# The places at which put-off layer-norm pieces are summed, moved to a list of 16 groups

## The chip, the cores and the metric

The kernel runs on one core of a Trainium2 chip. The metric is the device time of one execution in microseconds; the median of several runs counts. Lower is better.

## The reference, cut to what matters

Two layers are applied to four images of 64 x 64 tokens with 256 channels, in float32. Layer 0 is self-attention over the 4096 tokens of an image with 32 score channels and 128 value channels, a projection back and a residual. Layer 1 is an attention over triangles of token pairs, with 8 heads, then a residual with layer norm, an MLP with 512 hidden channels and a second layer norm.

```python
def _L0_conv_ref(x, Wf, bf, Wg, bg, Wh, bh, Wo, bo):
    f = xt @ Wf + bf
    g = xt @ Wg + bg
    v = xt @ Wh + bh
    s = jnp.einsum('bqd,bkd->bqk', g, f)
    beta = jax.nn.softmax(s, axis=-1)
    o = jnp.einsum('bqk,bkd->bqd', beta, v)
    o = o @ Wo + bo
    return x + o.reshape(b, h, w, c)

def _L1_conv_ref(...):
    ...
    out = jnp.einsum('biljh,bilhd,bljhd->bijhd', att, v1, v2)
    attn_out = out.reshape(B, N, N, E) @ Wo
    h = x_in + attn_out
    h = _layer_norm(h, ln_agg_g, ln_agg_b)
    mlp = jax.nn.relu(h @ W1 + b1) @ W2 + b2
    h = mlp + h
    return _layer_norm(h, ln_out_g, ln_out_b)
```

The change concerns the last two lines for images 0 and 1: the sum `mlp + h` and the layer norm after it.

## The kernel before

**Order of images.** `run` goes through images b = 0 to 3. For each it does layer 0 (`layer0`) and then layer 1 (`first_layer1` for image 0, `next_layer1` for the others). The order of instructions is the order in which the program issues them; each engine works off its own queue in that order, and an instruction waits at the head of its queue for semaphores of other engines. PE is TensorE, DVE is VectorE, ACT is ScalarE, POOL is GpSimd, SP is SyncE, which issues most DMAs.

**Put-off pieces.** Layer 1's tail (projection, layer norm, MLP) is done in pieces of 256 tokens, 16 an image (`NP`). While layer 1 of image b runs, the pieces of image b - 1 go through the matmuls of the tail. For images 0 and 1 the last part is put off: `carried_off` and `summed_off` store h and the MLP's output z in a DRAM tile `raw` (512 KB a piece, both together), and layer 0 of the image after next (b = 2 or 3) takes them up again. The last part of a piece has six steps, all methods of `Tokens`:

- `recall`: a tile `hz` in the ring of tag "R" (three buffers) is filled from `raw` by a DMA on SP (L1107).
- `settle`: on DVE, h times a row, plus a row, plus z (L1112 to L1114, 128 x 512 each), and statistics (L1185, L1186).
- `rooted`: on ACT, two small activations for one over the root (L1213, L1215).
- `polished`: on DVE, four small instructions that make scale and bias `rn` (L1225 to L1228).
- `scaled`: on ACT, two activations of 128 x 256 (L1247).
- `finish`: on POOL, two products of 128 x 512 (L1337, L1338), then the store to the output on SP (L1339).

**Layer 0.** The queries of an image are eight blocks (`qb`) of 512; the keys eight groups (`k`) of 512. The loop runs over 64 groups of scores g = 8 qb + k. In each group `values(g)` interleaves on PE four score matmuls of group g + 1 (L559, into pairs of PSUM banks; two pairs in all) with four o matmuls of group g (L586). ACT makes the exponentials of the scores in two instructions of 128 x 1024 (L571) into a buffer `e` (tag "k8", two buffers). DVE adds e to a running sum `esum` (L593; a copy, L591, where k = 0). At k = 7 DVE folds the sum together (L596 to L603) and splits it into two parts, `part`, in the ring of tag "hid" (one buffer).

The work on block qb - 1 is spread over the groups of block qb by a table `parts`: at k = 0 `norm` (den matmul on PE, L611; reciprocal on DVE, L615; `oT`, L617) and `bounds` (two reductions, L625), at k = 1 `output` (y, L639, and its stores), later the projections for layer 1, with copies on ACT (L672, L681, L706) into the ring of tag "st" and stores on SP. In image 3 `turn_y` follows at k = 5: eight transposes on DVE (L651) into a buffer of tag "hid", and four stores (L654).

The six steps of the put-off pieces come last in a group, and only where `b > 1`. Their places before:

```python
if b > 1:
    first = 3 * qb if qb < 2 else 2 + 2 * qb
    for t in range(3 if qb < 2 else 2 if qb < last else 0):
        for do, at in (
            (rest.recall, t), (rest.settle, 2 + t + t // 2), (rest.rooted, 3 + t + t // 2),
            (rest.polished, 4 + t + t // 2), (rest.scaled, 5 + t + t // 2), (rest.finish, 7),
        ):
            if k == min(at, 7):
                do(NP * (b - 2) + first + t)
```

So blocks 0 and 1 have three pieces each, settled at k = 2, 3 and 5, and blocks 2 to 6 two each, settled at k = 2 and 3.

Of the kernel before, what the change touches and what calls it, by code (L numbers as in the profile page):

```python
# [29 lines left out]
NP = T // 256  # L30
# [15 lines left out]
    A15/2 R00/1 A17/2 T10/2 A14/2 sp/1 R02/1 sa R05/1 e0/1 R01/1 z0/1 rr/1 T11/2 z1/1 pp/1 e1/1 so/1 A00/1 A05/1  # L46
    R07/1 W1/1 A02/1 A01/1 fa S1 ht V1/1 S0 hU hT
""".split()


ORDER_LAST = """
# [23 lines left out]
def attention_then_triangle_kernel(  # L75
# [99 lines left out]
    def add_b2():  # L175
        b2_bc = work.tile([P, C], F32, tag="st", name="b2_bc", bufs=3)
        nc.gpsimd.dma_start(out=b2_bc, in_=b2.partition_broadcast(P))
        nc.gpsimd.tensor_tensor(lb2_bc, lb2_bc, b2_bc, ALU.add)
        nc.gpsimd.tensor_tensor(lab2_sb, lab2_sb, lab_sb, ALU.add)
# [19 lines left out]
    def fold_bias():  # L199
        ps = pb("fold")  # L200
        for cc in range(2):
            nc.tensor.matmul(ps[:, cc : cc + 1], wo0_sb[:, 0, ts(cc, P)], bh_sb, start=True, stop=True)
        nc.vector.tensor_tensor(bo_sb, bo_sb, ps[:, 0:2], ALU.add)
# [7 lines left out]
    def limits(b):  # L211
        for j, op in enumerate((ALU.min, ALU.max)):
            nc.vector.tensor_reduce(lims[:, j, b : b + 1], dens, AX.X, op)
# [124 lines left out]
    class Ahead:  # L338
# [30 lines left out]
        def load(self, s):  # L369
            if s < self.n:  # L370
                for cc, (tag, bufs) in enumerate((("hT", 2), ("st", 3))):
                    t = self.xT[s, cc] = work.tile([P, 512], F32, tag=tag, name="xT", bufs=bufs)
                    nc.sync.dma_start(out=t, in_=self.d[1 + s // 8]["x"][ts(cc, P), ts(s % 8, 512)])
# [130 lines left out]
    def layer0(b, F, safe, rest, ahead):  # L504
# [14 lines left out]
        def max_piece(qc, t, mx):  # L519
            ps = pb("mxp")  # L520
            nc.tensor.matmul(ps, gT[qc // 16][:, ts(qc % 16, P)], fT[t // 4][:, ts(t % 4, 512)], start=True, stop=True)
            nc.vector.tensor_reduce(mx[:, qc % 4, t : t + 1], ps, AX.X, ALU.max)


        def max_row(mx):
            m = small.tile([P, 4], F32, tag="m", name="m")
            nc.vector.tensor_reduce(m, mx, AX.X, ALU.max)
            ps = pb("row")
            for n in range(4):
                nc.tensor.matmul(  # L530
                    ps[:, ts(n, P)], m[:, n : n + 1].to_broadcast([P, P]), ident, start=True, stop=True
                )
            row = work.tile([P, QB], BF16, tag="attP", name="row")
            nc.scalar.mul(row, ps, -1.0)
            return row

        def pieces(qb):
            mx = small.tile([P, 4, 8], F32, tag="mx", name="mx", bufs=2)
            return mx, [(qb * 4 + n, t) for n in range(4) for t in range(8)]
# [89 lines left out]
        def y(qb, cc):  # L629
            return yT[cc][:, ts(qb, QB)] if qb < last else stage[2][:, 2 + cc, :]  # L630
# [15 lines left out]
        def turn_y(qb, **where):  # L646
            t = work.tile([P, 16, 2, 32], F32, name="yr", **where)
            for cc in range(2):
                rows = y(qb, cc).rearrange("p (k t) -> p k t", t=32)
                for k in range(4):  # L650
                    nc.vector.transpose(t[:, ts(k, 4), cc, :], rows[:, ts(k, 4), :])  # L651
            def kept():
                for r in range(4):
                    nc.sync.dma_start(  # L654
                        out=io["yt"][ts(qb, QB), ts(r, 64)].rearrange("(k t) c -> t k c", t=32),
                        in_=t[ts(r, 32)].rearrange("t k h c -> t k (h c)"),
                    )
            return kept
# [5 lines left out]
        def proj(qb, name, m, ps=None, st=None, queue=nc.sync):  # L664
            col, rows = ts(qb, QB), ts(m, P)
            w = {"q": wq_sb, "k": wk_sb, "v2": wv2_sb}[name]
            ps = pb("proj") if ps is None else ps
            for cc in range(2):
                nc.tensor.matmul(ps, w[:, cc, rows], y(qb, cc), start=(cc == 0), stop=(cc == 1))  # L669
            st = staged(st)  # L670
            if name == "q":
                nc.scalar.mul(  # L672
                    st.rearrange("p (o i l) -> p i o l", o=2, l=32),
                    ps.rearrange("p (i o l) -> p i o l", o=2, l=32), scale1,
                )
                queue.dma_start(
                    out=io["q"][rows, :, ts(qb, 8), :].rearrange("c o i l -> c o (i l)"),
                    in_=st.rearrange("p (o x) -> p o x", o=2),
                )
                return  # L680
            nc.scalar.copy(st, ps)  # L681
            if name == "k":
                queue.dma_start(out=io["k"][rows, col], in_=st)
            else:
                queue.dma_start(
                    out=io["v2"][ts(qb, 8), rows, :].rearrange("l c j -> c l j"),
                    in_=st.rearrange("p (l j) -> p l j", j=N),
                )
# [8 lines left out]
        def proj1(qb, m, ps=None, st=None, queue=nc.sync):  # L697
            ps = pb("v1p") if ps is None else ps
            for n in range(2):
                for cc in range(2):  # L700
                    nc.tensor.matmul(  # L701
                        ps[:, ts(n, C)], y(qb, cc)[:, ts(m * 2 + n, P)], wv1_sb[:, cc, :],
                        start=(cc == 0), stop=(cc == 1),
                    )
            st = staged(st)
            nc.scalar.copy(st, ps)  # L706
            queue.dma_start(
                out=io["v1"][ts(qb * 2 + m, 256), :].rearrange("(n p) c -> p n c", p=P),
                in_=st.rearrange("p (n c) -> p n c", n=2),
            )  # L710
# [3 lines left out]
        def proj_qk(qk, st):  # L714
# [26 lines left out]
        parts = [  # L741
            [norm, bounds],
            [output],
            [lambda qb: proj(qb, "q", 0)],
            [lambda qb: proj(qb, "k", 0), lambda qb: proj(qb, "v2", 0)],
            [lambda qb: proj1(qb, 0)],
            [lambda qb: proj1(qb, 1), lambda qb: proj(qb, "q", 1)],
            [lambda qb: proj(qb, "k", 1)],
            [lambda qb: proj(qb, "v2", 1)],
# [5 lines left out]
            parts[6] = [lambda qb: proj(qb, "q", 1)]  # L755
            parts[7] = [lambda qb: proj(qb, "k", 1)]
        if turned_ahead(b):
            parts[5].append(lambda qb: turn_y(qb, tag="hid", bufs=1)())
        last = NQB - 1
        for r in range(4):  # L760
            score(0, r)
        for g in range(8 * NQB):
            qb, k = divmod(g, 8)
            if b == 0 and not safe:
                for load in later[3 * g : 3 * g + 3]:
                    load()
                if g == 6:
                    fold_bias()
                if g == 20:
                    add_b2()  # L770
            if safe and k == 0 and qb + 1 < NQB:
                mx, todo = pieces(qb + 1)
                for qc, t in todo:
                    max_piece(qc, t, mx)
                row[qb + 1] = max_row(mx)
            values(g, g + 1 < 8 * NQB)

            if qb > 0 and not (qb == last and k >= 6 + late):
                for part in parts[k]:
                    part(qb - 1)  # L780
            if late and g % 2 == 0 and 0 <= g // 2 - 2 < ahead.n:
                ahead.bring(g // 2 - 2)
            if late and g % 2 == 1 and 0 <= g // 2 - 3 < ahead.n:
                ahead.turn(g // 2 - 3)
            if b > 1:
                first = 3 * qb if qb < 2 else 2 + 2 * qb
                for t in range(3 if qb < 2 else 2 if qb < last else 0):
                    for do, at in (
                        (rest.recall, t), (rest.settle, 2 + t + t // 2), (rest.rooted, 3 + t + t // 2),
                        (rest.polished, 4 + t + t // 2), (rest.scaled, 5 + t + t // 2), (rest.finish, 7),  # L790
                    ):
                        if k == min(at, 7):
                            do(NP * (b - 2) + first + t)
            if g == 1 and b > 0 and not safe:
                limits(b - 1)
            if qb == last and k == 3:
                L.fetch_v1(0)
                L.fetch_v1(1)
            if qb == last and k == 5:
                if b > 0:  # L800
                    rest.load(NP * (b - 1))
                L.fetch_qk(0, True)
# [277 lines left out]
    def turned_ahead(b):  # L1080
        return b == NB - 1
# [652 lines left out]
```

## Time and profile before

| | |
|---|---|
| Median of 3 runs (lowest to highest) | 3637.06 us (3630.78 to 3638.11) |
| Time of the profiled execution | 3637.93 us |
| Its span, first to last instruction | 3636.1 us |
| Mean granted clock of TensorE | 0.993 |
| Busy: PE, DVE, ACT, POOL | 97%, 79%, 53%, 49% of the span |
| First to last o matmul (L586) of layer 0: images 0, 1, 2, 3 | 365.7, 386.9, 395.8, 394.4 us |
| settle's first instruction (L1112) | 32 times, median 685 ns, longest 1771 ns |
| finish on POOL (L1337, L1338) | 32 times each, medians 1279 and 1275 ns, longest 1805 and 3296 ns |

The span is the profiled execution's; the runs are timed without a profile. Busy shares are means over stages that differ, so the stage in which the changed code runs has to be read by itself: layer 0 of image 2 (its o matmuls from 1732.5 us on) and of image 3 (from 2600.9 us on). Image 1's layer 0 (from 872.7 us on) has the same matmuls and no put-off pieces.

### The profile page before, as it was taken

The page shows a single profiled execution, that of the slowest core. Times are in us where ns is not written, and L with a number is a line of the kernel's source. Part 1 is how long each engine was busy: PE and PEld are TensorE (multiplying, and loading weights), DVE is VectorE, ACT ScalarE, POOL GpSimd, SP SyncE. Part 2 cuts the span into 40 slices and gives each one's busy share as a digit, 9 for nine tenths or more (in the row PEclk, how much of TensorE's full clock was granted, in tenths as well). Part 3 has the DMA queues.
Part 4 walks back from the last instruction along what each step waited for, and adds up shares of the span by engine and source line. Part 5 has one row for each costly group of instructions (what it writes and reads, how often), then busy time and mean ns, then how long its engine had stood idle before and what let it go on. Part 6 is the DMA issues. An engine that isn't in the chain of part 4 may idle for free.

```text
span 3636.1 us, 58663 instructions
## 1 busy us (share of the span) xinstructions
PE 3521.2 (97%) x22218; PEld 1888.1 (52%) x22218; DVE 2862.1 (79%) x2662; ACT 1922.6 (53%) x4221; POOL 1770.2 (49%) x904
## 2 busy tenths in 40 slices
PE   9999999988999999999999999999899999999998
PEld 6555444434555555554455555554445555555477
DVE  4777499996555569999776649999887766999987
ACT  3444455544444366665444446666444446777655
POOL 5000199995000068989111118889611105999920
PEclk9999999999999999999999999999999999999999
DMA  9444555465111354425422254343623236431221
GB/s 175 140 129 124 138 148 142 117 138 130 50 52 49 90 137 107 104 65 107 112 90 85 75 142 112 85 107 73 138 93 99 90 92 152 97 92 50 66 69 57
DMA packets 509492, 374.37 MB, mean 103 GB/s; under 512 B 320080, under 2 KB 450896, under 8 KB 500368
## 3 DMA queue, kind: packets, MB, share of 16 engines
q1 hardware_dynamic: 460160, 343.56, 34.3%
q0 software_dynamic: 36160, 19.94, 5.4%
q10 hardware_dynamic: 12880, 7.01, 0.6%
q8 instruction: 178, 2.92, 0.3%
q14 instruction: 114, 0.93, 0.1%
HBM read 205.73 MB, written 164.63 MB: 102 GB/s over the span
## 4 chain that ended last, share of the span: by engine, by line
PE 64%; DVE 9%; POOL 6%; issue 4%; ACT 2%; DMA 2%; SPq 0%; ACTq 0%; DVEq 0%; POOLq 0%
PE acc L1052 17%; PE o L586 16%; PE proj L669 6%; POOL Rp L1042 6%; PE zp L1323 4%; PE s L559 4%; PE mp L1303 4%; DVE R L1042 4%; PE sp L940 3%; PE v1p L701 2%; PE hp L1160 2%; PE y L638 1%; PE att L994 1%; DVE esum L593 1%; DVE st L1185 1%
## 5 line engine op out<-in xcount | busy, mean ns | idle before, releaser
L1042 POOL TENSOR_TENSOR Rp<-attP,v 128x2048 f32<-128x2048 f32 x328 | 1491.5, 4578 | 410.1 <-ACT attP L1002 366.9
L1042 DVE TENSOR_TENSOR R<-att,v 128x2048 f32<-128x2048 f32 x696 | 1546.2, 2278 | 68.1 <-PE acc L1052 49.5
L586 PE MATMUL o<-e,v 128*128 128x512 f32 x2048 | 1046.9, 594 | 0.0
L593 DVE TENSOR_TENSOR esum<-esum,e 128x2048 f32<-128x2048 f32 x224 | 513.4, 2292 | 386.4 <-ACT e L571 384.5
L571 ACT ACTIVATE e<-s 128x1024 f32<-128x1024 f32 x512 | 522.4, 1023 | 539.8 <-PE s L559 436.8
L559 PE MATMUL s<-gT,fT 128*128 128x512 f32 x1024 | 786.0, 769 | 18.4 <-ACT e L571 14.8
L1052 PE MATMUL acc<-R,wsel 128*32 128x512 f32 x5568 | 706.8, 603 | 26.9 <-DVE R L1042 19.8
L586 PEld LDWEIGHTS o<-e,v 128*128 128x128 f32 x2048 | 388.7, 190 | 276.6 <-issue 233.9
L1062 ACT COPY ao<-acc 128x1024 f32<-128x1024 f32 x256 | 256.5, 1013 | 290.9 <-PE acc L1052 205.8
L1052 PE MATMUL acc<-Rp,wsel 128*32 128x512 f32 x2624 | 344.4, 596 | 22.8 <-POOL Rp L1042 20.3
L1052 PEld LDWEIGHTS acc<-R,wsel 128*32 128x32 f32 x5568 | 156.0, 110 | 396.2 <-issue 277.1
L1337 POOL TENSOR_TENSOR hz<-hz,log_bc 128x512 f32<-128x512 f32 x32 | 44.7, 1397 | 602.7 <-ACT hz L1247 602.7
L559 PEld LDWEIGHTS s<-gT,fT 128*128 128x128 f32 x1024 | 194.5, 190 | 258.7 <-issue 230.3
L977 ACT ACTIVATE es<-S,rd 128x64 f32<-128x64 f32 x1024 | 258.3, 337 | 15.0 <-DVE rd L969 13.1
L1231 POOL TENSOR_SCALAR nt<-mv 128x2 f32<-128x2 f32 (+1 forms) x49 | 9.4, 192 | 524.0 <-DVE mv L1186 518.9
L1303 PE MATMUL mp<-hT,w 128*128 128x256 f32 x1024 | 244.8, 384 | 1.7 <-ACT hT L1275 1.7
L1323 PE MATMUL zp<-w,hid 128*128 128x256 f32 x1024 | 240.0, 385 | 2.5 <-ACT hid L1312 2.1
L1323 PEld LDWEIGHTS zp<-w,hid 128*128 128x128 f32 x1024 | 187.9, 190 | 50.1 <-issue 14.7
L1303 PEld LDWEIGHTS mp<-hT,w 128*128 128x128 f32 x1024 | 185.1, 190 | 54.8 <-ACT attP L1002 12.6
L1052 PEld LDWEIGHTS acc<-Rp,wsel 128*32 128x32 f32 x2624 | 80.8, 110 | 210.8 <-issue 145.3
L615 DVE RECIPROCAL rec<-den 128x512 f32<-128x512 f32 x32 | 107.4, 3357 | 104.9 <-PE den L611 99.5
L950 ACT ACTIVATE S<-sp 128x512 f32<-128x512 f32 x128 | 131.5, 1093 | 77.9 <-PE sp L940 77.9
(195 smaller groups left out, 3705.1 us busy)
## 6 DMA issues: line engine op xcount, KB each, us to landing
v<-v2d SPq DMA_DIRECT2D x44, 512.0 KB
v1c<-v1d SPq DMA_DIRECT2D x128, 128.0 KB
aT<-ao SPq DMA_DIRECT2D x1024, 16.0 KB
A<-aT SPq DMA_DIRECT2D x256, 64.0 KB
hz<-raw SPq DMA_DIRECT2D x32, 512.0 KB
y<-yT SPq DMA_DIRECT2D x56, 256.0 KB
q<-st SPq DMA_DIRECT2D x56, 256.0 KB
k<-st SPq DMA_DIRECT2D x52, 256.0 KB
```

The lines of the kernel that those rows point to most:

```text
L559: nc.tensor.matmul(s_ps[r // 2][:, r % 2, :], fT[tt][:, ts(r * 4 + n, P)], gT[qb // 4][:, ts(qb % 4, QB)], start=True, stop=not safe,)
L571: nc.scalar.activation(e[g][:, 2 * j : 2 * j + 2, :], s_ps[j], AF.Exp)
L586: nc.tensor.matmul(o_ps[qb], F.v[tt][:, r * 4 + n, :], es[:, r, :], start=(k == 0 and r == 0), stop=(k == 7 and r == 3),)
L593: nc.vector.tensor_tensor(esum[qb], esum[qb], es, ALU.add)
L669: nc.tensor.matmul(ps, w[:, cc, rows], y(qb, cc), start=(cc == 0), stop=(cc == 1))
L950: nc.scalar.activation(self.S[pair][:, :, l0 : l0 + 8].rearrange("p i l -> p l i"), sp[:, lh], AF.Copy if self.safe else AF.Exp,)
L977: nc.scalar.mul(e[:, i, :], rows[:, i, :], rec[:, i : i + 1])
L1042: eng.tensor_tensor(R, src.unsqueeze(1).to_broadcast([P, D, N]), v2[h], ALU.mult)
L1052: nc.tensor.matmul(acc[32 * c : 32 * c + 32, n % 2, :], w[:, n, c, 16 * h : 16 * h + 32], R[:, ts(c, 8), :].rearrange("p d j -> p (d j)"), ...
L1062: nc.scalar.copy(self.ao[step][:, ts(np, 2)].rearrange("p k d j -> p k (d j)"), self.acc[step][np])
L1303: nc.tensor.matmul(self.mp[:, fc % 2, :], w1_sb[:, cc, ts(fc, P)], self.hT[tt][:, cc, :], start=(cc == 0), stop=(cc == 1),)
L1323: nc.tensor.matmul(zp[:, n, :], self.hid[tt][:, fc, ts(n, P)], w2_sb[:, fc, :], start=(fc == 0), stop=(fc == 3 and tt not in self.hT2),)
```

## The change

A list `SETTLED` names the group g, 0 to 63, in which each of the 16 pieces is settled. The other steps are placed relative to it: `recall` three groups earlier, `rooted`, `polished`, `scaled` and `finish` one, two, three and four groups later, across block boundaries. Block 0 has one piece, and blocks 1 to 6 have three and two in turn. In blocks with three, k is 2, 4 and 6; in blocks with two it is 2 and 5; in block 0 it is 5. The last piece is finished in group 57. Besides, `turn_y` (image 3) moves from the work of k = 5 to that of k = 3.

```diff
+SETTLED = [5, 10, 12, 14, 18, 21, 26, 28, 30, 34, 37, 42, 44, 46, 50, 53]
...
         if turned_ahead(b):
-            parts[5].append(lambda qb: turn_y(qb, tag="hid", bufs=1)())
+            parts[3].append(lambda qb: turn_y(qb, tag="hid", bufs=1)())
...
-            if b > 1:
-                first = 3 * qb if qb < 2 else 2 + 2 * qb
-                for t in range(3 if qb < 2 else 2 if qb < last else 0):
-                    for do, at in (
-                        (rest.recall, t), (rest.settle, 2 + t + t // 2), (rest.rooted, 3 + t + t // 2),
-                        (rest.polished, 4 + t + t // 2), (rest.scaled, 5 + t + t // 2), (rest.finish, 7),
-                    ):
-                        if k == min(at, 7):
-                            do(NP * (b - 2) + first + t)
+            for do, after in (
+                (rest.recall, -3), (rest.settle, 0), (rest.rooted, 1), (rest.polished, 2), (rest.scaled, 3), (rest.finish, 4),
+            ):
+                if b > 1 and g - after in SETTLED:
+                    do(NP * (b - 2) + SETTLED.index(g - after))
```

## The prediction

> **What bounds the kernel now.** The first part of the page says that TensorE (PE) is the bound of nearly every stage:
>
> ```profile
> PE 3521.2 (97%) x22218; PEld 1888.1 (52%) x22218; DVE 2862.1 (79%) x2662; ACT 1922.6 (53%) x4221; POOL 1770.2 (49%) x904
> ```
>
> PE stands idle only 3636.1 - 3521.2 = 114.9 us, so a change that takes no matmul away can win only idle time of PE, or time at a lowered clock. I therefore looked for idle PE where the diff acts: layer 0 of images 2 and 3, which alone settle put-off pieces (`b > 1`). Image 1's layer 0 runs the same matmuls in the same order and settles nothing: it is the yardstick. I read from the timeline when each of the 64 groups of scores starts its first o matmul (L586), and asked for the windows from group 1 to group 10, then from group 10 to group 63, for images 1, 2 and 3 (columns: stretch, its length, then busy us and instructions of each engine):
>
> ```profile
> 878.50:919.90 41.40, 41.40 (x116) 21.52 (x115) 27.28 (x19) 18.92 (x19) 0.00 (x0) 1.00 0.17 67
> 1738.30:1788.60 50.30, 44.33 (x116) 21.85 (x115) 42.85 (x54) 22.87 (x31) 10.18 (x6) 0.97 0.30 117
> 2606.70:2655.60 48.90, 43.99 (x116) 21.92 (x115) 42.82 (x54) 22.97 (x31) 10.16 (x6) 0.97 0.30 121
> ...
> 919.90:1256.60 336.70, 336.70 (x944) 178.23 (x943) 175.07 (x116) 139.97 (x160) 0.00 (x0) 1.00 0.16 55
> 1788.60:2125.30 336.70, 336.70 (x944) 178.24 (x943) 231.37 (x257) 156.55 (x212) 36.53 (x26) 1.00 0.26 84
> 2655.60:2992.30 336.70, 336.70 (x944) 178.26 (x943) 241.69 (x313) 156.52 (x212) 36.51 (x26) 1.00 0.30 93
> ```
>
> The last three rows are equal to the hundredth: from group 10 on, settling costs PE nothing. The first three differ: 50.30 - 41.40 = 8.90 us for image 2 and 48.90 - 41.40 = 7.50 us for image 3, at the end of the first block of 512 queries. In image 3, groups 7, 8 and 9 take 6.75, 8.16 and 7.75 us against 4.35, 4.82 and 6.15 in image 1.
>
> What PE waits for there is in image 3's timeline, by engine (start, us, engine, line, what; in brackets the idle time and what ended it):
>
> ```profile
> 2639.34 0.50 PE L559 MATMUL s<-gT,fT 128*128 128x512 f32 x1 [2.13 <-ACT e L571]
> 2644.81 0.50 PE L611 MATMUL den<-part,ones_f 128*128 128x512 f32 x1 [0.59 <-DVE part L603]
> 2647.50 0.50 PE L559 MATMUL s<-gT,fT 128*128 128x512 f32 x1 [2.19 <-ACT e L571]
> ```
> ```profile
> 2638.27 1.94 ACT L571 ACTIVATE e<-s 128x1024 f32<-128x1024 f32 x2 [1.70 <-DVE esum L593]
> 2645.45 1.09 ACT L1247 ACTIVATE hz<-hz,rn 128x256 f32<-128x256 f32 x2 [5.25 <-DVE rn L1228]
> ```
>
> Three idle stretches, and behind each is VectorE. The exponential at 2638.27 waits until a running sum (esum) frees the older of two e buffers. The den matmul waits for the parted sums. The third is scaling: its ACTIVATE stood 5.25 us at the head of ScalarE's queue, as piece 2's polish and scaling both fall in group 7 and the polish is queued behind the end-of-block sums; two exponentials stand behind it, and PE behind those. Then the clock is lowered, which these windows show (eighth column, PEclk):
>
> ```profile
> 2648.00:2651.40 3.40, 3.40 (x7) 1.38 (x5) 3.37 (x4) 1.39 (x2) 1.23 (x1) 0.50 0.34 94
> 1781.10:1784.40 3.30, 3.30 (x6) 1.34 (x4) 3.27 (x4) 1.27 (x2) 1.12 (x1) 0.50 0.38 108
> ```
>
> So the excess in image 3 is 0.59 + 2.13 + 2.19 = 4.91 us idle, the rest mainly slow matmuls.
>
> [...] L1338 on POOL takes 1.27 us alone and 3.29 us beside esum at 2636.00; the y sums (L639, one input in PSUM) stay at 741 to 752 ns.
>
> **The change, part by part.** No matmul, and no instruction on any engine, is added or taken away; 32 pieces (16 an image) move in time.
>
> *One settle.* By image 3's timeline the first runs from 2616.12 to 2619.47: 3.35 us of VectorE. A polish is 2644.68 to 2645.42, 0.74 us, and the two products of finish 1.27 + 1.27 us of POOL. A group needs one esum of 2.29 us; in block 0 a group is 4.35 us, so 2.06 us are free (that is the gap ahead of each esum in image 1), in a later block 6.07 to 7.79 less 2.29, 3.8 to 5.5 us.
>
> *Block 0, before.* Settles in groups 2, 3 and 5, three polishes by group 7: 3 x 3.35 + 3 x 0.74 = 12.3 us, mostly in five groups with 5 x 2.06 = 10.3 us free, plus POOL's products, which hold VectorE up (L1112 took 1.77 and L1227 1.21 us). VectorE reaches the block's end late.
>
> *Block 0, after: one piece, settled in group 5.* On image 1's times: esum(5) ends at 898.30, the settle at 901.65; esum(6), ready at 900.36, ends at 903.94 in place of 902.65. The exponential that needs that buffer starts at 905.82: 1.88 us to spare. Esum(7) is on time (904.71). The sums end at 910.31, the polish at 911.05, the next copy of 1.22 at 912.3; the reciprocal was due at 913.67, so 1.4 us remain. Scaling now falls in group 8, after its polish, so ScalarE doesn't wait; the products then run under the reciprocal. All three idle stretches go, and the clock's drop with them: **-8.90 and -7.50 us**.
>
> *Later blocks: two or three pieces, never in neighbouring groups.* They settle at k = 2, 4 and 6 or at k = 2 and 5; now it is k = 2, 3 and 5 or 2 and 3. New is k = 6 (pieces of groups 14, 30, 46). On image 2's block that begins at 1879: esum(6) ends at 1916.94, the settle at 1920.30, the polish of the piece from k = 4 by 1922.8 at most[...]. Esum(7) started at 1922.45: 0.35 us late, so the block's last sum ends by 1928.4. In the profile it ends at 1930.08, held by products that now run later, and the reciprocal still waits 3 to 4 us for den. The products of the piece from k = 4 then run at about 1931.1 to 1933.7, ahead of the next reciprocal at 1934.9. A polish at k = 7 (the settle of k = 5) is there today in block 1, and group 16 is no longer for it. Cost 0.
>
> *New at a block's start: a polish after norm and bounds* (for the settle at k = 6). It pushes esum(1) and the y sums by 0.74 us. Image 1 shows what covers it: the exponential after esum(1) ends at 1023.90 and PE reuses its PSUM pair at 1026.93, 3.0 us; the first y sum ends at 1023.44 and its projection starts at 1025.62, 2.2 us. That piece's products then meet esum(2) and may delay it by 2.54 us; its reader has about 4 us. From below 0, from above a stop of 0.3 us (0.74 + 2.54 - 3.0, were both to fall on esum(1)) at each of six places, 2 us in all. I take 0.
>
> *turn_y moved from k = 5 to k = 3, image 3 only.* Eight transposes (2777.81 to 2779.47, 1.66 us) come after esum in a group of 7.78 us, and the settle of a neighbouring group ends before it. Its four stores pass, on SP, the v1 and q stores that they stood behind; the hid buffer is wanted back only at k = 7. 0.
>
> *SP's queue.* The same 32 recalls and 32 output stores, spread: a recall comes three groups ahead of its settle (in block 0 over 13 us; the profile shows the first landing about 10 us after its issue), and its R buffer was finished at least one group before. A recall that waits for that store holds up only stores of st, of which three are in flight. 0.
>
> Sum: -8.90 - 7.50 = **-16.4 us**. The profiled execution took 3637.93 us with 3636.1 of span and becomes 3621.5; the median of the runs stands 0.87 us lower: 3637.06 - 16.4 = **3620.7**.
>
> **Rivals.**
> - *Half of it.* The settle in block 0's short groups still costs a stop with its clock drop. For it: 2.06 us free against 3.35. A stop of 2.1 us and 1.6 us at half clock (group 9: 7.75 - 6.15), in each image: 7.4 us kept, 3628.1. Against it: 1.88 us to spare above.
> - *Nothing.* The stops come from late transfers: L1112 waited 4.0 and 2.65 us for its recall. If the one piece still comes when block 0 ends, 3637. Against it: PE waits for VectorE and ScalarE by name, and group 5 gives the recall 18 us.
> - *Slower.* The settle at k = 6 does to six block turns (groups 14, 30, 46, in two images) what block 0's bunch does to one. The price is that turn's in image 3: 2.40 + 3.34 + 1.60 = 7.3 us. Six are 44, less 16.4: +27.6, 3664.7. It decides once VectorE comes to the sums later than the 3.6 to 5.1 us for which the reciprocal now waits; I found 0.35.
>
> **How the numbers follow.** The runs spread over 7.3 us, 0.2% of the time, which is also about the least that a measurement of this kernel can tell from no change (line: 3629.8). Forecast 0.73, within 5 us; half 0.13, mostly under the line; nothing 0.07; slower 0.07. From 3613 (8 us below the forecast, for more clock drops saved in later stages) to 3630 nearly all of the first two cases lies inside. Faster 0.83, same 0.09, slower 0.08.
>
> **What would show it.** The windows from group 1 to group 10 of images 2 and 3 at 41.4 us, PE busy throughout, PEclk 1.00; no idle of PE ahead of den; no ACTIVATE of L1247 waiting 5 us for rn; groups 10 to 63 still 336.7 us. Windows over 337 with idle at blocks' turns would prove the slower rival; a stop in groups 6 to 9, the half.

## The result, and the profile after

| | before | after |
|---|---|---|
| Median (lowest to highest), 6 runs each | 3636.08 us (3630.78 to 3638.11) | 3622.58 us (3618.24 to 3623.49) |
| Span of the profiled execution | 3636.1 us | 3621.6 us |

The ratio is 0.9963, with a 95% interval of 0.995 to 0.9975: 9 to 18 us faster. The forecast was 3620.7 us.

The page after says that PE's work is unchanged and its idle time is smaller, 3621.6 - 3516.2 = 105.4 us against 114.9:

```profile
PE 3516.2 (97%) x22218; PEld 1887.8 (52%) x22218; DVE 2849.8 (79%) x2662; ACT 1923.5 (53%) x4221; POOL 1777.1 (49%) x904
```

The same windows as in the prediction, from group 1 to group 10 and from group 10 to group 63 of layer 0, for images 1, 2 and 3 (stretch, length, busy us of PE, PEld, DVE, ACT and POOL, then PEclk):

```profile
880.20:921.60 41.40, 41.40 (x116) 21.53 (x115) 27.24 (x19) 18.94 (x19) 0.00 (x0) 1.00 0.17 68
1740.10:1781.50 41.40, 41.40 (x116) 21.54 (x115) 30.81 (x30) 20.38 (x23) 2.54 (x2) 1.00 0.24 98
2599.80:2641.20 41.40, 41.40 (x115) 21.53 (x114) 30.75 (x30) 20.45 (x23) 2.55 (x2) 1.00 0.24 99
...
921.60:1258.30 336.70, 336.70 (x944) 178.27 (x943) 175.06 (x116) 139.82 (x160) 0.00 (x0) 1.00 0.16 55
1781.50:2118.20 336.70, 336.70 (x944) 178.24 (x943) 237.68 (x281) 159.81 (x220) 47.12 (x30) 1.00 0.28 89
2641.20:2978.00 336.80, 336.80 (x945) 178.31 (x944) 247.79 (x337) 159.85 (x220) 47.13 (x30) 1.00 0.33 100
```

Images 2 and 3 now run block 0 and its turn in image 1's time, with PE busy throughout and PEclk at 1.00. The 0.1 us in the last row is rounding of the window's ends; from the start times themselves all three are 336.75 us. VectorE shows how much room is left at the turn of image 2's block 0, in its timeline (start, us, engine, line, what, idle before it):

```profile
1772.40 0.16 DVE L1228 SCALAR_TENSOR_TENSOR rn<-mv,rn 128x2 f32<-128x2 f32 x1
1772.48 1.23 DVE L595 COPY esum<-e 128x2048 f32<-128x2048 f32 x1
1775.27 3.36 DVE L619 RECIPROCAL rec<-den 128x512 f32<-128x512 f32 x1 [1.56 <-PE den L615]
```

VectorE waits 1.56 us for PE here; before, PE waited for VectorE. In image 2 the stage lost 50.31 - 41.40 = 8.91 us before, in image 3 48.93 - 41.40 = 7.53, now nothing: 16.4 us. The spans differ by 14.45. The other 2.0 us lie in code that the change doesn't touch: 1.3 of them before image 0's first o matmul, around which the clock stood at half (PEclk 0.50) for 6.8 us against 3.4. Single executions scatter by more than that (after: 3618.24 to 3623.49).

### The profile page after: what moved, and what is told of

Its sections match the earlier page's. It is cut to its first block, busy times and chain, and to the rows that moved or that the text cites. A ratio compares the mean times of both kernels' runs of the same rounds, so it can differ in the third digit from the quotient of the medians.

```text
span 3621.6 us, 58681 instructions
## 1 busy us (share of the span) xinstructions
PE 3516.2 (97%) x22218; PEld 1887.8 (52%) x22218; DVE 2849.8 (79%) x2662; ACT 1923.5 (53%) x4221; POOL 1777.1 (49%) x904
## 4 chain that ended last, share of the span: by engine, by line
PE 68%; POOL 7%; DVE 6%; issue 4%; ACT 2%; DMA 0%; SPq 0%; ACTq 0%; DVEq 0%; POOLq 0%
PE o L590 18%; PE acc L1052 17%; PE proj L673 6%; POOL Rp L1042 6%; PE s L563 5%; PE mp L1303 5%; PE zp L1323 5%; PE sp L940 3%; DVE R L1042 3%; PE v1p L705 2%; PE hp L1160 2%; PE y L642 1%; PE att L994 1%; PE htp L1270 1%; PE hp L1166 0%
## 5 line engine op out<-in xcount | busy, mean ns | idle before, releaser
L590 PE MATMUL o<-e,v 128*128 128x512 f32 x2048 | 1043.7, 592 | 0.0
L575 ACT ACTIVATE e<-s 128x1024 f32<-128x1024 f32 x512 | 522.9, 1023 | 532.4 <-PE s L563 447.6
L590 PEld LDWEIGHTS o<-e,v 128*128 128x128 f32 x2048 | 388.3, 190 | 276.7 <-issue 233.8
L1337 POOL TENSOR_TENSOR hz<-hz,log_bc 128x512 f32<-128x512 f32 x32 | 45.6, 1426 | 599.9 <-ACT hz L1247 599.9
L619 DVE RECIPROCAL rec<-den 128x512 f32<-128x512 f32 x32 | 107.4, 3357 | 126.5 <-PE den L615 121.2
```

The costliest lines, as they stand in the source:

```text
L575: nc.scalar.activation(e[g][:, 2 * j : 2 * j + 2, :], s_ps[j], AF.Exp)
L590: nc.tensor.matmul(o_ps[qb], F.v[tt][:, r * 4 + n, :], es[:, r, :], start=(k == 0 and r == 0), stop=(k == 7 and r == 3),)
```

## Experiments

All lists keep the rule that a piece is recalled only after the piece three before it has been finished. Where a list begins at k = 2, the recall is clipped to group 0; the loop then goes over the list by number, so that two pieces can also share a group. A single execution can lie some 6 us off its kernel's median (before: 3631.11 to 3643.12 in 34), so runs with only one are read from their windows. In the changed kernel the lines ahead of the loop over groups stand four higher than before (L586 is L590, L611 is L615, L615 is L619, L638 is L642, L571 is L575), and in the runs with a clipped recall or two settles in a group those after the loop one higher (L1112 is L1113, L1337 is L1338). "Excess" is the time from group 1 to group 10 over image 1's 41.4 us.

### Neighbouring groups in the later blocks

```diff
-SETTLED = [5, 10, 12, 14, 18, 21, 26, 28, 30, 34, 37, 42, 44, 46, 50, 53]
+SETTLED = [5, 10, 11, 13, 18, 19, 21, 26, 27, 29, 34, 35, 42, 43, 50, 51]
```

> Theory A (load of block 0): only the number of pieces in the first block matters, neighbours later are free, so this is the changed kernel's time, 3622.6 us within 3, with 41.4 us from group 1 to 10 and 336.7 us from group 10 to 63 in images 2 and 3. Rival N (neighbours): settles in neighbouring groups cost PE time wherever they stand; five blocks with a pair in each of two images, at 1 to 2 us a pair, give 3632 to 3642 us, and the excess lies after group 10.

Median 3619.19 us, ratio to before 0.9931 to 0.9964: not to be told from the changed kernel. The windows of images 2 and 3, in the order of the last fence:

```profile
1742.74:1784.14 41.40, 41.40 (x116) 21.52 (x114) 30.78 (x30) 20.47 (x23) 2.54 (x2) 1.00 0.27 110
2602.86:2644.25 41.39, 41.39 (x115) 21.53 (x114) 30.77 (x30) 20.47 (x23) 2.56 (x2) 1.00 0.27 111
1784.14:2120.89 336.75, 336.75 (x945) 178.27 (x944) 239.91 (x281) 159.51 (x220) 42.50 (x30) 1.00 0.27 88
2644.25:2981.01 336.76, 336.76 (x945) 178.27 (x944) 250.75 (x337) 159.50 (x220) 42.51 (x30) 1.00 0.32 98
```

Six blocks of each image have a pair of neighbours here (the expectation counts five), and none costs PE anything: "never neighbours" is worth nothing after block 0.

### Three pieces in the first block, spread

```diff
-SETTLED = [5, 10, 12, 14, 18, 21, 26, 28, 30, 34, 37, 42, 44, 46, 50, 53]
+SETTLED = [2, 4, 6, 10, 12, 14, 18, 21, 26, 28, 34, 37, 42, 44, 50, 53]
```

> Three pieces in the first block, but at k = 2, 4 and 6. Theory A: VectorE has 2.06 us free in a group and needs 3 x 3.35 us for settles and 0.74 us for each polish before the block's end, so den's matmul comes late by some 4 us and the clock drops (1.6 us): 5 to 6 us an image, 3632 to 3635 us. Rival N: no two are neighbours, so no stop: 3622.6 us. Rival Q (queue): the loss came from polish and scaling of piece 2 in one group; here they are one group apart, so at most 2 us an image, 3622.6 to 3626.5 us.

Median 3636.15 us, ratio 0.9987 to 1.0004: the whole gain is gone. The excess is 8.6 us in image 2 and 7.3 in image 3. Image 2's timeline shows the stop, and a window the clock behind it (0.50):

```profile
1779.24 0.72 PE L615 MATMUL den<-part,ones_f 128*128 128x512 f32 x1 [4.05 <-DVE part L605]
1780.57 0.80 PE L615 MATMUL den<-part,ones_f 128*128 128x512 f32 x1 [0.60 <-DVE part L607]
```
```profile
1779.30:1786.10 6.80, 6.20 (x10) 3.24 (x11) 6.73 (x6) 1.02 (x1) 0.00 (x0) 0.50 0.11 39
```

Theory A's stop of about 4 us at den came as 4.05 (3.42 in image 3). What was too small in my 5 to 6 us was the clock, at half for 6.8 us and not 3.4, so the median lies above the 3632 to 3635 us. The last settle now stands at k = 6, right ahead of the block's sums, and the second piece's products, by their place in the list, meet these sums: in image 2 L600 takes 2.17 us in place of 1.23. Three pieces don't fit at k = 2, 4 and 6 either. Rivals N and Q fall.

### Three pieces bunched as before, scaling one group after its polish

```diff
-SETTLED = [5, 10, 12, 14, 18, 21, 26, 28, 30, 34, 37, 42, 44, 46, 50, 53]
+SETTLED = [2, 3, 5, 10, 12, 14, 18, 21, 26, 28, 34, 37, 42, 44, 50, 53]
```

> Three pieces in the first block at k = 2, 3 and 5 as before, but the third one's scaling one group after its polish. Theory A: the first two stops of before stay (2.13 + 0.59 us and the clock's drop, 1.6 us), the third shrinks: 4 to 5 us an image, 3631 to 3633 us. Rival Q: the third stop was most of it, so 2 us an image or less, up to 3626.5 us. Rival N: everything stays, 3637 to 3639 us.

Median 3635.71 us, ratio 0.9985 to 0.9999. The excess is 6.8 and 5.5 us, 2.1 us less in each image than before: more than the 4 to 5 us of theory A, less than the whole that rival N gave, and far over rival Q's 2 us. Image 3 (the last line is cut off by the end of its window):

```profile
2631.66 0.50 PE L563 MATMUL s<-gT,fT 128*128 128x512 f32 x1 [1.90 <-ACT e L575]
2636.76 0.49 PE L615 MATMUL den<-part,ones_f 128*128 128x512 f32 x1 [0.49 <-DVE part L605]
2638.09 0.50 PE L615 MATMUL den<-part,ones_f 128*128 128x512 f32 x1 [0.83 <-DVE part L607]
2643.89 1.55 PE L642 MATMUL y<-oT,wo 128*128 128x512 f32 x3 [0.95 <-DVE oT L621]
```

The stop of 2.19 us ahead of group 9 is gone. In its place y waits 0.95 us for oT, which it had hidden: VectorE is late all the same.

Most of the 2.1 us is the clock, which cost group 9 of the kernel before 1.6 us. Here it never dropped in image 3 (PEclk 1.00 from group 1 to 10), and in image 2 it dropped inside group 8. The windows of group 8 in images 2 and 3 show that this drop cost nothing: the group took as long at full clock, with PE idle for 1.3 us of it (PEclk is the third column from the end):

```profile
1766.68:1773.33 6.65, 6.65 (x16) 3.28 (x15) 6.44 (x10) 2.56 (x3) 2.87 (x1) 0.74 0.11 39
2633.36:2640.02 6.66, 5.34 (x15) 2.56 (x14) 6.45 (x11) 3.21 (x5) 1.66 (x2) 1.00 0.11 39
```

So with the products still there, scaling one group later is by itself worth about half a microsecond an image (estimates: 8.9 - 1.6 against 6.8, 7.5 - 1.6 against 5.5).

### Two pieces in the first block

```diff
-SETTLED = [5, 10, 12, 14, 18, 21, 26, 28, 30, 34, 37, 42, 44, 46, 50, 53]
+SETTLED = [2, 5, 10, 12, 18, 21, 26, 28, 30, 34, 37, 42, 44, 46, 50, 53]
```

> Two pieces in the first block, at k = 2 and 5. Theory A, worked out from image 1's times: the first settle's backlog is gone by group 4; its products on POOL hold esum(6) and esum(7) up to about 905.2 and 907.5, the block's sums end at 910.8, polish and copy at 912.8, ahead of the reciprocal at 913.67. No stop: 3622.6 us. If VectorE's spare time is smaller than that (rival: even two are too many), a stop with its clock drop of 2 to 4 us an image: 3627 to 3631 us.

Median 3619.86 us, ratio 0.9937 to 0.997. The excess is 0.5 us in image 2 and 0 in image 3. The first line below is VectorE in image 2, behind a recall that had not landed; the second is VectorE at the turn of image 3's block 0:

```profile
1743.30 0.69 DVE L1113 TENSOR_TENSOR hz<-hz,lag_bc 128x512 f32<-128x512 f32 x1 [4.07 <-DMA hz<-raw]
```
```profile
2628.09 3.36 DVE L619 RECIPROCAL rec<-den 128x512 f32<-128x512 f32 x1 [0.45 <-PE den L615]
```

Two pieces fit, with 0.45 us to spare in place of 1.56 (0.25 in image 2). And a settle at k = 2 is early enough to meet its transfer: VectorE waits, and image 2's group 4 loses 0.5 us. Settling first at k = 5 also avoids that.

### turn_y alone

```diff
-            parts[5].append(lambda qb: turn_y(qb, tag="hid", bufs=1)())
+            parts[3].append(lambda qb: turn_y(qb, tag="hid", bufs=1)())
```

> The kernel before with turn_y alone moved from k = 5 to k = 3. My account gives the move nothing: the time of before, 3636.1 us within 3, with 50.3 and 48.9 us from group 1 to 10. Rival: part of the gain is this move's (the hid buffer or VectorE's work at k = 5), then image 3's blocks 1 to 7 are shorter than 336.7 us, and the time lower by over 3 us.

Median 3635.99 us against 3636.44 beside it, ratio 0.999 to 1.0009; image 3 has 48.96 us from group 1 to 10 and 336.75 from there on. The move is worth nothing, as forecast.

### The kernel before without POOL's products

```diff
-            eng.tensor_tensor(z, z, log_bc.unsqueeze(1).to_broadcast([P, 2, C]), ALU.mult)
-            eng.tensor_tensor(z, z, lob_bc.unsqueeze(1).to_broadcast([P, 2, C]), ALU.add)
+            if b > 1:
+                eng.tensor_tensor(z, z, log_bc.unsqueeze(1).to_broadcast([P, 2, C]), ALU.mult)
+                eng.tensor_tensor(z, z, lob_bc.unsqueeze(1).to_broadcast([P, 2, C]), ALU.add)
```

> The kernel before, without the two products of finish on POOL for the put-off pieces (this part of the last layer norm is left out). Theory P [...]: in block 0 POOL's products hold VectorE up by about 3.0 us (L1227 1.05, L1112 1.08, esum 0.9), just what makes it too late; without them the first two stops go and the third shrinks to 0.5 us or less: at most 1 us an image in place of 7.5 to 8.9, 3620 to 3624 us. Theory A alone (load of the settles): 3 us of some 8 are saved in each image, 3629 to 3632 us. [...]

Median 3632.53 us, ratio 0.9982 to 0.9995. The excess is 5.9 and 3.2 us, so 3.0 and 4.3 us were saved. The clock did not drop in image 3 this time (PEclk 1.00 from group 1 to 10), which is some 1.6 of its 4.3 us, so both are about the 3 us of theory A, and theory P falls. (The medians differ by 3.9 us, with an interval of 1.8 to 6.5. In the profiled execution 1.9 us came back after the last arithmetic: counted from the last o matmul, the last store was issued at 635.3 us against 635.4 before, and the program ended at 642.6 against 640.7.) In image 3 the stop ahead of group 7 is nearly gone, the one ahead of group 9 is not, and ScalarE again waits for rn:

```profile
2641.03 0.50 PE L559 MATMUL s<-gT,fT 128*128 128x512 f32 x1 [2.19 <-ACT e L571]
```
```profile
2638.98 1.09 ACT L1247 ACTIVATE hz<-hz,rn 128x256 f32<-128x256 f32 x2 [4.37 <-DVE rn L1228]
```

### Both: no products, and scaling one group later

The list `[2, 3, 5, 10, ...]` of the bunched run, with the products left out as in the last diff.

> Three pieces at k = 2, 3 and 5 in the first block, the third's scaling one group after its polish, and the two products of finish for the put-off pieces left out (that part of the last layer norm is not computed). My account: [...] with both away image 3 loses at most 1.2 us from group 1 to 10 and image 2 at most 3 us (it keeps its late transfer, 1.6 us). If the mere load of three settles decides, 3 us stay in image 3 and 5 in image 2.

A single execution: 3625.53 us, beside 3637.38 before. The excess is 3.1 and 1.7 us, a little over what I allowed (3 and 1.2). What remains at the turn is one wait of y:

```profile
2641.06 1.98 PE L642 MATMUL y<-oT,wo 128*128 128x512 f32 x4 [0.95 <-DVE oT L621]
```

Image 3's 7.5 us are thus taken apart: without the products the excess is 3.2, without the order of polish and scaling 5.5, without both 1.7. That last part is the load of three settles and polishes alone. Of these four kernels only the one before has the clock's drop in image 3 (PEclk 0.97 from group 1 to 10, against 1.00 in the other three). Without its 1.6 us the four figures are 5.9, 3.2, 5.5 and 1.7: the order is worth about 0.4 us beside the products and 1.5 without them, since one lateness of VectorE hides behind the other. The shares don't add up.

### Two neighbours in the first block

```diff
-SETTLED = [5, 10, 12, 14, 18, 21, 26, 28, 30, 34, 37, 42, 44, 46, 50, 53]
+SETTLED = [2, 3, 10, 12, 18, 21, 26, 28, 30, 34, 37, 42, 44, 46, 50, 53]
```

> Two pieces in the first block, in neighbouring groups, at k = 2 and 3. Theory A (what counts is that VectorE has caught up by the block's end): the early groups lose what they lost before, 0.2 us in image 3 and 1.5 us in image 2 (groups 4 and 5, behind a late transfer), and the turn nothing: 41.6 and 42.9 us from group 1 to 10. If neighbours cost by themselves, a stop at the turn with its clock drop comes on top: over 44 us.

A single execution: 3623.64 us. From group 1 to 10 image 3 took 43.5 us and image 2 44.9, where the run with settles at k = 2 and 5 took 41.4 and 41.9. Theory A gave 41.6 and 42.9, so it is wrong here; the rival's stop at the turn came, but without a drop of the clock (PEclk 1.00 from group 1 to 10 in both images). The early groups lost 0.6 us in image 3 and 2.0 in image 2, the turn 1.5 us in each. In image 3 VectorE's sum and POOL's second product meet just ahead of it:

```profile
2629.66 2.18 DVE L600 TENSOR_TENSOR esum<-esum 128x1024 f32<-128x1024 f32 x1
```
```profile
2625.53 1.95 POOL L1338 TENSOR_TENSOR hz<-hz,log_bc 128x512 f32<-128x512 f32 x1 [1.33 <-ACT hz L1248]
2627.55 3.20 POOL L1339 TENSOR_TENSOR hz<-hz,lob_bc 128x512 f32<-128x512 f32 x1
```

I had followed the settles to the turn and not the second piece's products, which begin once its scaling is done, three groups later. The sum took 2.18 us in place of 1.23 and den's second matmul waited 0.75. So in the short groups of block 0 the number of pieces doesn't decide alone: at two pieces, neighbouring settles cost 2.1 us in image 3 and 3.0 in image 2.

### Settles at k = 7, one and two

```diff
-SETTLED = [5, 10, 12, 14, 18, 21, 26, 28, 30, 34, 37, 42, 44, 46, 50, 53]
+SETTLED = [5, 10, 12, 15, 18, 21, 26, 28, 31, 34, 37, 42, 44, 47, 50, 53]
...
+SETTLED = [5, 10, 15, 15, 18, 23, 26, 31, 31, 34, 39, 42, 47, 47, 50, 55]
```

The first list is the run with one, the second that with two in a group.

> The changed kernel with the settles of groups 14, 30 and 46 put at k = 7, behind the block's sums. In the changed kernel the reciprocal waits 5.0 to 5.1 us for den at those turns; settle takes 3.35 us of it, so no stop: 3622.6 us, with the reciprocal's wait down to 1.5 to 1.8 us. The slower rival of the prediction (work near a turn stops PE) would give 2 to 7 us at each of six turns: 3634 to 3665 us.

Median 3620.62 us, ratio 0.9944 to 0.9972. No excess; at the turn after block 1 the reciprocal waits 2.41 us, which is more room than the 1.5 to 1.8 us I gave it.

> Two settles at k = 7 of blocks 1, 3 and 5, one at k = 7 of blocks 2, 4 and 6. By the reciprocal's wait of 5.0 to 5.1 us: one settle fits (3.35), two (6.7) are 1.4 us too many with the gaps, so the reciprocal, oT and the y matmuls come 1.4 us late at six turns: 8 to 9 us, 3631 us, more if the clock drops too (up to 3640). If the slack is not what the wait shows (a store or a buffer hides it), no change: 3622.6 us.

Median 3626.18 us, ratio 0.9956 to 0.9981. From group 10 to 63 images 2 and 3 take 2.3 us longer, 0.77 us at each of three turns, all of it here:

```profile
1829.91 1.98 PE L642 MATMUL y<-oT,wo 128*128 128x512 f32 x4 [0.57 <-DVE oT L621]
```

The place is right, the size half (4.6 us in all, not 8 to 9): two settles back to back took 6.5 us, and the reciprocal came some 0.8 us late, not 1.4. The spare time of later blocks is real, and it ends where the profile says.

### One piece, but at k = 7 of the first block

```diff
-SETTLED = [5, 10, 12, 14, 18, 21, 26, 28, 30, 34, 37, 42, 44, 46, 50, 53]
+SETTLED = [7, 10, 12, 15, 18, 21, 26, 28, 31, 34, 37, 42, 44, 47, 50, 53]
```

> One piece in the first block, but settled at k = 7, behind the block's sums, where the profile of the changed kernel leaves the reciprocal 1.56 us beyond a polish (2.2 us in all). From image 1's times: sums end at 910.3, settle at 913.6, copy at 914.8, the reciprocal was due at 913.7. So even one piece stops PE here: 1.0 us in each image (42.4 us from group 1 to 10), at the y matmuls, and the turns of later blocks stay free. If the number alone decided, 41.4 us.

A single execution: 3625.85 us; the excess is 0.93 us in each image, at y, with 336.75 us from group 10 on (its later settles at k = 7 cost nothing, as in the run above). Where the one piece stands decides too.

## Why the prediction was right

- **The place and the size.** The two gains, -8.90 and -7.50 us, came as -8.91 and -7.53. The medians moved by 13.5 us, and the interval of 9 to 18 holds the 16.4.
- **Block 0's working.** I found 1.4 us to spare ahead of the reciprocal; the profile after has 1.56. Scaling one group behind its polish was given as the cure of the third stop: the bunched run shows that stop gone, but a wait for oT in its place, so that the cure alone is worth about half a microsecond. The forecast did not hang on it, as one piece in place of three ended every wait.
- **What did it.** The prediction named the bunch's load, POOL's products and the same-group polish and scaling together, and did not weigh them. The runs do: in image 3, 1.7 us remain with the load alone, and the other two, with the clock's drop that only the kernel with both shows there, bring it to 7.5. Nor is the load the number of pieces alone: two fit at k = 2 and 5, not at k = 2 and 3, and one does not fit at k = 7.
- **Later blocks at 0.** Right: 336.75 us with settles at k = 6, in neighbouring groups, or at k = 7. I gave the reciprocal a wait of 3 to 4 us; it is 5.0 to 5.1, as the products no longer meet the block's sums (at image 2's turn after block 1 the last product before them ends at 1813.84, the last esum starts at 1813.97).
- **The polish at a block's start.** It costs PE nothing, as I took. I had not followed it to ScalarE: there, at six turns, scaling waits 1.48 us at the head of the queue. The exponential behind it would have waited for esum anyway (the second line):

```profile
1832.10 1.09 ACT L1247 ACTIVATE hz<-hz,rn 128x256 f32<-128x256 f32 x2 [1.48 <-DVE rn L1228]
1834.31 1.02 ACT L575 ACTIVATE e<-s 128x1024 f32<-128x1024 f32 x1 [1.12 <-DVE esum L597]
```

- **The products and the next sums.** The prediction let the products delay esum(2) by up to 2.54 us. In the profile after it is POOL's product that takes longer: beside esum at 1835.45, which takes its usual 2.28 us, the second product takes 3.42 us in place of 1.27.
- **A reading that proved nothing.** The prediction set the y sums' 741 to 752 ns beside the 3.29 us that L1338 took next to esum. In layer 0 of images 2 and 3 before, no y sum runs beside a product, so these figures could not show what a product does to a y sum. In the profile after 12 of them do, and take 740 to 746 ns; no forecast here hangs on that.
- **turn_y and SP's queue.** The move of turn_y alone changed nothing. Of the recalls I said that block 0 gives them time; the two-piece run shows that this is worth 0.5 us in image 2.
- **The rivals.** "Nothing" (late transfers) fits part of image 2's loss: before, image 2 lost 1.4 us more than image 3, all of it in groups 4 and 5, behind a first settle that waited 4.0 us for its transfer, against 2.65 in image 3. The two-piece run gives 0.5 us for such a wait alone; no run took the wait away and left three pieces, so the rest stays open. "Slower" needed VectorE over 3.6 us late at a later turn; even two settles at k = 7 were only about 0.8 us too many.

## What to carry to other kernels

Where a bound engine runs the same instructions with and without some side work, compare the two stretches group by group: the difference is the most that moving the side work can bring, and it also shows where moving it is free. Count the side work against the free time of the shortest groups first, with the room left at the next point where the bound engine waits for a result. Don't place two steps of one chain in the same group when the second heads another engine's queue (scaling stood there for 5.25 us); but expect little from ending one such wait (here about half a microsecond an image) while the engine behind it is still late, as the next late result takes its place.

## What the runs showed of the hardware that I had not expected

- **The clock after a stop.** The length of one stop did not tell whether a drop followed. In image 3 a stop of 2.19 us with one of 0.59 just before was followed by 3.4 us at half clock in the kernel before (PEclk 0.50 in 2648.0 to 2651.4); the same 2.19 us in the run without products, at 2641.03 and with no stop ahead of den, were followed by none (PEclk 1.00 in 2641.0 to 2644.4). Nor was there a drop in image 3 of the bunched run, with stops of 1.90, 0.49 and 0.83 us (PEclk 1.00 from group 1 to 10). What decides between them was not shown.
- **How long it lasted.** In the run with three pieces spread, half clock came with image 2's stops of 4.05 and 0.60 us and lasted 6.8 us (PEclk 0.50 in 1779.3 to 1786.1), against 3.4 us at image 2's turn in the kernel before (0.50 in 1781.1 to 1784.4).
- **What it cost.** That hung on what PE did meanwhile: 1.6 us in group 9 of the kernel before, where PE was busy throughout (3.40 of 3.40 us), nothing in group 8 of the bunched run's image 2, which took 6.65 us against 6.66 at full clock in image 3. The spread three pieces stopped PE for 4.05 + 0.60 us at image 2's turn, and its groups 8 and 9 took 8.0 us more.
